# Output slots of a store-bound pairwise product: four of 83 pairs in place of three of 124

## The chip, the cores and the metric

One core of a Trainium2 chip. The metric is the device time of one execution in microseconds (us). "The profile" is one execution recorded by the hardware profiler; "the packet records" are the trace's list of single DMA packets with start, duration, size and queue (it does not name the engine), from which I worked out what the views do not show.

## The reference

For 4,096 rows of 32 fields of 64 numbers, each field is multiplied by one 64x64 matrix, and every pair (i, j) of fields with i < j gives a product, element by element: 496 pairs a row, 520 MB of fp32 output from 34 MB of input.

```python
def reference(r_x, L0_rec_W):
    vid = jnp.einsum('bfd,de->bfe', x, W)
    idx_i, idx_j = jnp.triu_indices(32, k=1)
    return x[:, idx_i, :] * vid[:, idx_j, :]
```

## The kernel before

The 4,096 rows are 16 tiles of 256. A tile's input is 128 partitions x 32 fields x 128 numbers; its output 128 partitions x 496 pairs x 128 numbers, 512 bytes a pair and partition. TensorE makes `vid`, VectorE multiplies, SyncE's queue stores, and ScalarE's queue loads the next tile in four DMAs of 512 KB. The first stores are cut by the list GROWING, since VectorE has no lead over the DMA yet.

```python
SLOT = 124
GROWING = [21, 15, 19, 23, ...]          # (cut) pairs of each early store
xpool = tc.tile_pool(name="x", bufs=2)   # (cut) two input tiles
opool = tc.tile_pool(name="out", bufs=3) # (cut) three output slots
...
def load(t, pieces, queue):
    xt = xpool.tile([P, F, C], F32, tag="x", name=f"x_{t}")
    n = F // pieces
    for lo in range(0, F, n):
        queue.dma_start(out=xt[:, lo : lo + n, :], in_=x[t][:, lo : lo + n, :])
    return xt
loaded = [load(0, 4, nc.sync), load(1, 2, nc.sync)]
...
for t in range(NT):
    if 0 < t < NT - 1:
        loaded.append(load(t + 1, 4, nc.scalar))
    ...                                  # matmuls of tile t into 8 PSUM banks
    for j in range(1, F):
        i = 0
        while i < j:
            at = first(j) + i
            base = at - at % SLOT
            if at == base:
                ot = opool.tile([P, SLOT, C], F32, tag="o", name=f"o_{t}_{at}")
            n = min(j - i, base + SLOT - at)
            nc.vector.tensor_tensor(ot[:, at - base : at - base + n, :], ...)
            i += n
            at += n
            if t * NP + at == until or at in (base + SLOT, NP):
                nc.sync.dma_start(out=out[t][:, sent:at, :],
                                  in_=ot[:, sent - base : at - base, :])
                sent = at
                ...                      # until += next(growing)
```

A store moves one row per partition. In the packet records each row is one packet: 63,488 bytes for 124 pairs, 128 packets a store. Each DMA also leaves 16 packets of 4 bytes and 9 ns (2,320 for the 145 DMAs of a run), which I take for the completions of the 16 DMA engines; so I count 8 rows of a store for each engine. A load packet is 4,096 bytes (8 fields).

## Time and profile before

| | before |
|---|---|
| time, median of the first 3 runs | 1298.64 us (1297.97 to 1299.37) |
| stores / later loads | 82 / 56 |
| VectorE busy | 1098.1 us |
| moved | 553.81 MB, 427 GB/s over the span |

The prediction shows the lines that say what bounds the kernel. One more view: the windows of the last microseconds. Columns: stretch and its length, busy time of PE, weight loads, VectorE and POOL, the clock, the busy share of the DMA engines, GB/s.

```profile
1280.00:1284.00 4.00, 0.00 (x0) 0.00 (x0) 0.00 (x0) 0.00 (x0) 0.50 0.88 381
1284.00:1288.00 4.00, 0.00 (x0) 0.00 (x0) 0.00 (x0) 0.00 (x0) 0.50 0.22 95
1288.00:1292.00 4.00, 0.00 (x0) 0.00 (x0) 0.00 (x0) 0.00 (x0) 0.50 0.15 63
1292.00:1296.00 4.00, 0.00 (x0) 0.00 (x0) 0.00 (x0) 0.00 (x0) 0.50 0.07 32
```

A share of 0.07 is about one engine of 16. Half of the engines are done by 1284 us, and for another 11 us the run waits for the others, in the end for two or one. By the packet records the 16 engines write their completions of the last store between 1282.9 and 1295.1 us. I call the difference between first and last, 12.2 us, the **spread**, and the amount by which the slowest engine ends after the mean of the 16 its **lag**, 9.1 us here. (The prediction's 1283.7 and 1295.9 are the same completions, counted from a zero 0.8 us earlier than the profile's. It also calls "lag" what is here the spread, as do the expectations ahead of the runs.)

### The profile page before, as it was taken

To read this page: it belongs to the slowest core of one execution; us is meant where nothing else is said; L and a number is where in the kernel's file an instruction comes from. 1 tells how busy PE (TensorE), PEld (TensorE's weight loads), DVE (VectorE), ACT (ScalarE), POOL (GpSimd) and SP (SyncE) were. 2 spreads that over 40 slices of the span, in tenths; PEclk is the share of its full clock that TensorE was granted. 3 is DMA by queue.
4 is the path that set the end of the run, shared out by engine and by line. 5 is a ranking of instruction groups with operands and counts; after the bars stand their busy time and mean duration, and the time that the engine had idled before them with its cause. 6 is when DMAs were issued, how large, how long until landed. Compare 5 with 4: busy or idle time off the path is not lost.

```text
span 1296.3 us, 2062 instructions
## 1 busy us (share of the span) xinstructions
PE 225.5 (17%) x512; PEld 52.1 (4%) x512; DVE 1098.1 (85%) x544; POOL 0.2 (0%) x4
## 2 busy tenths in 40 slices
PE   4112131122121121211212112121121211212000
PEld 1000000000000000000000000000000000000000
DVE  7999999898798888988888888888888888979970
POOL 0000000000000000000000000000000000000000
PEclk8555555565555555655555565555555655555555
DMA  9999999999999999999999999999999999999996
GB/s 379 430 426 433 438 432 425 434 434 434 428 432 432 434 432 434 431 434 436 432 434 434 426 434 432 430 432 432 432 433 431 434 432 434 432 431 443 425 431 288
DMA packets 20891, 553.81 MB, mean 427 GB/s; under 512 B 2448, under 2 KB 2448, under 8 KB 10256
## 3 DMA queue, kind: packets, MB, share of 16 engines
q1 hardware_dynamic: 12816, 524.33, 93.8%
q10 hardware_dynamic: 8064, 29.36, 5.5%
q8 instruction: 4, 0.07, 0.0%
q14 instruction: 7, 0.06, 0.0%
HBM read 33.59 MB, written 520.09 MB: 427 GB/s over the span
## 4 chain that ended last, share of the span: by engine, by line
DMA 61%; DVE 34%; issue 1%; DVEq 0%; PE 0%; SPq 0%
DMA out_dram<-o 61%; DVE o L99 34%; DMA x<-in_r_x_dram 0%; DVEq L145 0%; PE pv L81 0%; DVEq L99 0%; SPq L56 0%
## 5 line engine op out<-in xcount | busy, mean ns | idle before, releaser
L99 DVE TENSOR_TENSOR o<-x,pv 128x2176 f32<-128x2176 f32 (+27 forms) x544 | 1098.1, 2093 | 158.3 <-DMA out_dram<-o 149.5
L81 PE MATMUL pv<-x,w 64*64 64x512 f32 x512 | 225.5, 1025 | 966.3 <-DMA x<-in_r_x_dram 887.2
L81 PEld LDWEIGHTS pv<-x,w 64*64 64x64 f32 x512 | 52.1, 208 | 1138.0 <-issue 1137.4
L128 POOL MEMSET const-bfloat16-1.0<- 128x1 bf16 x1 | 0.1, 102 | 0.0
L128 POOL MEMSET const-uint8-127<- 128x1 uint8 x1 | 0.1, 102 | 0.0
L128 POOL MEMSET const-float32-1.0<- 128x1 f32 x1 | 0.1, 99 | 0.0
L128 POOL MEMSET const-float32-0.0<- 128x1 f32 x1 | 0.1, 98 | 0.2 <-issue 0.2
## 6 DMA issues: line engine op xcount, KB each, us to landing
out_dram<-o SPq DMA_DIRECT2D x56, 7936.0 KB, 42.9
x<-in_r_x_dram ACTq DMA_DIRECT2D x56, 512.0 KB, 48.7
out_dram<-o SPq DMA_DIRECT2D x2, 3008.0 KB, 17.8
out_dram<-o SPq DMA_DIRECT2D x1, 5952.0 KB, 27.1
out_dram<-o SPq DMA_DIRECT2D x1, 4928.0 KB, 23.1
out_dram<-o SPq DMA_DIRECT2D x1, 4416.0 KB, 19.0
out_dram<-o SPq DMA_DIRECT2D x1, 4224.0 KB, 21.2
out_dram<-o SPq DMA_DIRECT2D x1, 3904.0 KB, 15.3
```

The source lines that it names most:

```text
L81: nc.tensor.matmul(pv[half, :, :], lhsT=w2[half, :], rhs=xt[half, b : b + BANK, :], start=True, stop=True,)
L99: nc.vector.tensor_tensor(ot[:, at - base : at - base + n, :], xt[:, i : i + n, :], vid[j // BANK][:, j % BANK : j % BANK + 1, :].to_broad ...
L128: nc = _bacc.Bacc("TRN2", target_bir_lowering=False, num_devices=1, dynamic_dma_scratch_size=1024)
```

## The change

It cuts the output into slots of 83 pairs, of which four take less memory than the three before (332 pairs against 372), and re-cuts the early stores. Its evident intent is a finer flow: VectorE waits for smaller stores, with more of them in flight.

```diff
-SLOT = 124
+SLOT = 83
 GROWING = [
-    21, 15, 19, 23, 27, 19, 29, 18, 19, 20, 38, 28, 24, 25, 47, 34, 29, 61,
-    55, 69, 66, 58, 77, 47, 93, 31,
+    21, 24, 21, 17, 22, 15, 16, 30, 24, 20, 21, 18, 27, 24, 32, 46, 37, 50,
+    31, 45, 38, 53, 30, 65, 18,
 ]
-    opool = ctx.enter_context(tc.tile_pool(name="out", bufs=3))
+    opool = ctx.enter_context(tc.tile_pool(name="out", bufs=4))
```

## The prediction

> **What bounds the kernel now.** I read the page first (slices, chain, groups), then the waits, then windows of the run's two ends, and last the trace's records of single DMA packets.
>
> ```profile
> DVE  7999999898798888988888888888888888979970
> DMA  9999999999999999999999999999999999999996
> GB/s 379 430 426 433 438 432 425 434 434 434 428 432 432 434 432 434 431 434 436 432 434 434 426 434 432 430 432 432 432 433 431 434 432 434 432 431 443 425 431 288
> DMA 61%; DVE 34%; issue 1%; DVEq 0%; PE 0%; SPq 0%
> L99 DVE TENSOR_TENSOR o<-x,pv 128x2176 f32<-128x2176 f32 (+27 forms) x544 | 1098.1, 2093 | 158.3 <-DMA out_dram<-o 149.5
> ```
>
> Each column is 32.4 us. The DMA engines are full in all but the last; VectorE is busy in eight or nine tenths, and nearly all its idle time (149.5 of 158.3 us) ends when a store of an earlier output slot lands. The chain of waits says 34% VectorE, but that is how the chain is followed (slot freed, multiply, store, next landing). VectorE is not the limit: it waits for slots that the DMA empties.
>
> ```profile
> 100.00:232.00 132.00, 26.05 (x56) 5.38 (x56) 130.92 (x65) 0.00 (x0) 0.53 1.00 431
> 232.00:1200.00 968.00, 174.42 (x384) 40.66 (x384) 824.15 (x409) 0.00 (x0) 0.54 1.00 433
> 1200.00:1256.00 56.00, 0.00 (x0) 0.00 (x0) 51.41 (x20) 0.00 (x0) 0.50 1.00 435
> 1280.00:1296.00 16.00, 0.00 (x0) 0.00 (x0) 0.00 (x0) 0.00 (x0) 0.50 0.33 143
> ```
>
> These are windows: stretch, length, PE, weight loads, VectorE, POOL, clock, DMA share, GB/s. Up to 232 us VectorE computes without a break and builds its lead (the sized first stores); from 232 us on 144 us of 968 are waits. The DMA share is 1.00 to 1280 us, then a third. In the packet records all 16 DMA engines have a packet in flight at every moment from 13 to 1280 us. The last store's 16 completions run from 1283.7 to 1295.9 us: eleven engines finish by about 1286, two at 1295. So **the end is set by the slowest of 16 always busy DMA engines**: its bytes, its packets, and the stalls peculiar to it.
>
> The sum for a fast engine: 553.65 MB / 16 = 34.60 MB. A 63,488-byte packet takes 2,342 ns (median), one of 4,096 bytes 159 ns, so 36.76 ps a byte plus 8.5 ns. On one engine a packet starts 3 to 4 ns before the one ahead has ended, so the pitch has about 5 ns a packet; after a store's last packet the next starts some 6 ns later than otherwise (completion write). 34.60 MB x 36.76 ps = 1272.0 us; (82 stores + 62 loads + weights) x 8 packets x 5 ns = 5.8; 145 completions x 6 ns = 0.9; first bytes at 3.0; slow first loads 1.4 (21.9 us of excess over 16 engines before 33 us). Together 1283.1 us, against 1283.7 measured. The slowest engine adds 12.2 us.
>
> [...] a tile's four loads (issued together on the other queue, 32 packets of 4 KB per engine) take up to 82.1 us to land, which is 32 x (2.342 + 0.159) = 80 us, one small packet behind each large one. So loads are always in flight in the plateau. [...] 133.3 ns a pair and 148 ns fixed, of which 60 ns are pitch, as the next instruction starts 88 ns before the end.
>
> **The change, part by part.**
>
> *Stores.* The order comparison shows 30 more rows on SyncE: 112 stores against 82 (64 whole slots become 96; the sized ones are cut differently). Same bytes. Each engine handles 30 x 8 = 240 more packets x 5 ns = 1.2 us, and 30 completions x 6 ns = 0.2 us. This is on the path: **+1.4 us**.
>
> *VectorE.* A tile is cut at five borders, not three, so 32 more multiplies (544 to 576 in all): busy time 1098.1 + 32 x 0.148 = 1102.8 us; on the clock 32 x 60 ns = 1.9 us. All of it comes out of the 149.5 us of waiting: **0**.
>
> *Slots.* Buffered pairs 3 x 124 = 372 become 4 x 83 = 332. Today VectorE starts a slot when the store three back lands, with two stores (40 us, at 20.0 us each with a load in flight) still queued, and issues 17.1 us later. A fast engine, 12 us ahead, has 40 - 12 - 17.1 = 11 us of work left then. After: a slot takes VectorE 17.1 x 83/124 = 11.4 us; a packet 42,496 x 36.76 ps + 8.5 = 1,570 ns, a store 8 x (1.570 + 0.159) = 13.8 us with a load behind each packet, 12.6 without. Three queued are about 40 us; left for a fast engine 40 - 12 - 11.4 = 17 us. The queue runs dry in neither: **0**.
>
> *Loads.* 32 x 1.729 = 55 us to land instead of 80, then 25 us of each tile without a load. They were in time already (VectorE waits 8.8 us for PE in the whole run, all at the start): **0**.
>
> *First stores.* The first (21 pairs) is the same, issued at 12.18 us, first packet 13.25: 1.07 us from issue to packet. The second ends at pair 45 instead of 36: the multiply of 9 pairs ends at 15.55 (14.20 + 1.348), so its packet can start at 16.65; the engines run dry at 16.46 (where store two starts today). **Up to 0.2 us** is lost. The next: pair 66 ends at 18.47, so 19.57, and the queue lasts to 16.65 + 24 x 0.151 = 20.3. Going on so, with 0.133 us per pair + 0.06 per instruction for VectorE and 0.151 per pair for the DMA, the slack stays above 0.7 us to the end of the sized stores, from the third mostly more than before's (down to 0.2 us at its fifth).
>
> *Tail.* When VectorE ends, three full slots are left to drain today (1256.4 to 1295.9). After, four smaller ones. It ends when the bytes are out: **0**.
>
> Sum without the slow engines: 1298.64 + 1.4 + 0.2 = **1300.2 us**.
>
> *Slowest engine.* This is the term I can't derive. The spread between first and last completion of a store is 1.0 us at 76 us, 1.4 at 172, then grows to 12.7 at 1170, about 0.2 us per store, and stays flat (12.2) in the last stores, where no load runs; it did not grow before 76 us either, where none ran. [...] Three readings: it goes with load packets (same number: 0); with store issues during loads (6 x 55/80 = 4.1 a tile against 4: 0, or x1.5 = +6 us if any issue counts); with bytes stored while loads fly (x0.69: -3.5 us). I choose +1: **1301 us**.
>
> **The rivals.**
> - *Starvation takes the place of slot waits.* Against: the slacks above, and 16 of 16 engines busy in the present profile with less reserve. If the sized stores were wrong, each hole costs its length, 1 to 5 us in all.
> - *Per-store overhead counts in full* [...] Against: today's sized stores, small and many, run at 426 to 433 GB/s (the first columns), so a store behind another costs almost nothing.
> - *Finer slots let VectorE work earlier and shorten the run.* It does start each piece earlier, but what it produces waits in the queue; its 149.5 us of waiting are the sign of a lead, not of loss. Worth 0.
> - *The stalls follow the packet length or the issues*: -3.5 to +6 us, the main spread.
>
> **Range and chances.** Low: 1300.2 - 3.5 = 1296.7; high: 1300.2 + 6 = 1306. I take 1296.5 to 1306. The 2% borders are 1272.7 and 1324.6; below the first lies less than the sum of a fast engine alone, above the second only a cost that today's small stores don't show. Faster 0.01, same 0.97, slower 0.02.
>
> **What would show it.** Right: DMA slices at nine to the end; 112 store issues; plateau near 433 GB/s; VectorE busy about 1103 us with 140 to 160 us of waits for stores in more and shorter pieces; load pieces landing at some 14, 28, 42, 55 us (median 35); a hole of at most 0.3 us near 16.5; the last store's completions spread over 8 to 18 us. Wrong: a slice below nine in mid run, a plateau below 428 GB/s, VectorE waiting on PE for more than 20 us, or a first stretch with engines without packets.

The numbers of the kernel before's profile behind these steps: VectorE takes 2,948 ns for 21 pairs and 4,281 ns for 31, which gives the 133.3 ns a pair and 148 ns fixed; where it does not wait, the next instruction starts 81 to 87 ns (median 83, where the prediction has 88) before the end of the one ahead. Of 6,045 load packets between 232 and 1180 us, 88% start 2 to 5 ns before a store packet ends and 4% the same time before another load packet ends, so the two kinds take turns. That many stores behind each other cost little beyond their packets was an estimate of mine from the 426 to 433 GB/s of the early, small ones. And 200 of the 6,064 store packets of 63,488 bytes in that stretch took over 50 ns longer than the line of 36.76 ps a byte plus 8.5 ns (2.39 to 2.91 us, median 2.48); a store was issued during 36% of these 200, and during 11% of all.

## The result, and the profile after

The changed kernel took **1295.02 us** (median of 4 runs, 1294.66 to 1297.10) against 1298.76 for the kernel before; ratio 0.9975, 95% interval 0.9958 to 0.9992. Ratios here are the mean time of one kernel's fast runs over that of the other's of the same rounds, so not quite the ratio of the medians quoted. A second comparison, told below, gave 1295.07 against 1298.09, ratio 0.9979 (0.9964 to 0.9995). So the change is worth about 3 us, a quarter of a per cent. At the 2% border that is "the same", as predicted, but the time lies below the range of 1296.5 to 1306, and the sign was wrong.

First the page's slices, chain and main group of the changed kernel:

```profile
DVE  7999999888898888988888888888888888888970
DMA  9999999999999999999999999999999999999998
GB/s 376 427 410 434 434 433 434 431 433 431 434 431 433 431 432 433 432 431 435 432 431 433 432 435 426 437 427 433 434 430 435 430 431 436 428 436 431 438 431 348
DMA 66%; DVE 29%; issue 1%; DVEq 0%; PE 0%; SPq 0%
L99 DVE TENSOR_TENSOR o<-x,pv 128x640 f32<-128x640 f32 (+14 forms) x576 | 1102.4, 1984 | 151.3 <-DMA out_dram<-o 142.2
```

Nothing has moved between engines: the DMA is full to the last slice, VectorE is busy 1102.4 us (predicted 1102.8) and waits 142.2 us for stores (predicted 140 to 160). The plateau is at nearly the same GB/s. What differs is the last slice, 348 GB/s against 288, and the third, 410 against 426. The windows of the changed kernel, for the same stretches as the prediction's and for the end:

```profile
100.00:232.00 132.00, 22.86 (x48) 4.46 (x48) 128.76 (x69) 0.00 (x0) 0.50 1.01 433
232.00:1200.00 968.00, 177.92 (x384) 38.06 (x384) 833.05 (x435) 0.00 (x0) 0.53 1.00 432
1200.00:1256.00 56.00, 0.00 (x0) 0.00 (x0) 49.69 (x20) 0.00 (x0) 0.50 1.00 432
...
1280.00:1284.00 4.00, 0.00 (x0) 0.00 (x0) 0.00 (x0) 0.00 (x0) 0.50 0.96 415
1284.00:1288.00 4.00, 0.00 (x0) 0.00 (x0) 0.00 (x0) 0.00 (x0) 0.50 0.65 280
1288.00:1292.00 4.00, 0.00 (x0) 0.00 (x0) 0.00 (x0) 0.00 (x0) 0.50 0.12 52
```

The plateau is a hair slower (432 against 433 in the long window), and the engines are busy longer: 0.65 against 0.22 between 1284 and 1288 us. But then it is over, where before a few engines still worked until 1295. The packet records say the same in single numbers:

| completions of the last store, us | first | mean of 16 | last | spread | lag |
|---|---|---|---|---|---|
| before | 1282.9 | 1286.1 | 1295.1 | 12.2 | 9.1 |
| after | 1285.7 | 1287.8 | 1291.9 | 6.2 | 4.1 |
| after, second profile | 1285.4 | 1288.0 | 1292.9 | 7.5 | 5.0 |

The average engine ends 1.7 to 1.9 us **later**, as the sum of the prediction said (+1.4 for packets, +0.2 for the start). The slowest ends 2.2 to 3.2 us **earlier**, because its lag has halved. The run ends with the slowest. So the question for the experiments: why do a few engines fall behind, and what in the change makes them fall behind less?

One local loss is visible too. These are windows from 90 to 95 us, first of the kernel before:

```profile
90.00:95.00 5.00, 2.01 (x6) 0.85 (x8) 5.00 (x5) 0.00 (x0) 0.50 0.99 422
```

and of the changed one:

```profile
90.00:95.00 5.00, 3.68 (x8) 0.85 (x8) 5.00 (x4) 0.00 (x0) 0.57 0.99 346
```

The DMA share is the same 0.99 with a fifth less moved: packets took longer. I count as **excess** what a packet took beyond 8.5 ns + 36.76 ps per byte, the line through the medians of 4,096 bytes (159 ns) and 63,488 bytes (2,342 ns). Between 33 and 100 us it is 1.9 us per engine after against 0.7 before. That is the third slice's 410 GB/s; every profile of the changed kernel's slots shows 1.6 to 1.9 us there, and why these packets are slow stays open.

### The profile page after: what moved, and what is told of

The parts are those of the page before. It is cut to its first block, busy times and chain, and to the rows that moved or that the text cites. A ratio compares the mean times of both kernels' runs of the same rounds, so it can differ in the third digit from the quotient of the medians.

```text
span 1293.3 us, 2181 instructions
## 1 busy us (share of the span) xinstructions
PE 229.0 (18%) x512; PEld 49.5 (4%) x512; DVE 1102.4 (85%) x576; POOL 0.2 (0%) x4
## 4 chain that ended last, share of the span: by engine, by line
DMA 66%; DVE 29%; issue 1%; DVEq 0%; PE 0%; SPq 0%
DMA out_dram<-o 65%; DVE o L99 29%; DMA x<-in_r_x_dram 0%; DVEq L145 0%; PE pv L81 0%; DVEq L99 0%; SPq L56 0%
## 5 line engine op out<-in xcount | busy, mean ns | idle before, releaser
L99 DVE TENSOR_TENSOR o<-x,pv 128x640 f32<-128x640 f32 (+14 forms) x576 | 1102.4, 1984 | 151.3 <-DMA out_dram<-o 142.2
L81 PE MATMUL pv<-x,w 64*64 64x512 f32 x512 | 229.0, 1027 | 951.7 <-DVE o L99 500.2
L81 PEld LDWEIGHTS pv<-x,w 64*64 64x64 f32 x512 | 49.5, 205 | 1129.5 <-issue 1124.8
## 6 DMA issues: line engine op xcount, KB each, us to landing
x<-in_r_x_dram ACTq DMA_DIRECT2D x56, 512.0 KB, 31.9
```

The source lines that it names most:

```text
L81: nc.tensor.matmul(pv[half, :, :], lhsT=w2[half, :], rhs=xt[half, b : b + BANK, :], start=True, stop=True,)
```

## The experiments

There were two ways to read the halved lag: by what the change did to the *slots* (four, smaller), or by what it did to the *packets* (42.5 KB instead of 63.5 KB). And there were the loads, since in the kernel before the spread grew only while loads were running. I name kernels by their slots ("124" before, "83" after) and the edit.

### No later loads, on 124

The two tiles loaded first are used in turn. The result is wrong on purpose.

```diff
-            loaded.append(load(t + 1, 4, nc.scalar))
+            loaded.append(loaded[(t + 1) % 2])
```

> The kernel before with no loads after the first two tiles (the two loaded tiles are used in turn; the result is wrong on purpose). 56 loads fewer take 29.36 MB / 16 x 36.76 ps + 56 x 46 ns = 70 us off every engine. Theory L: the spread of the last store's completions is 1 to 2 us instead of 12.2, time about 1218 us, more than 70 us less. Theory S or I: spread about 12, 1228 us.

Measured in one look: 1220.42 us. Its windows at the end:

```profile
1208.00:1212.00 4.00, 0.00 (x0) 0.00 (x0) 0.00 (x0) 0.00 (x0) 0.50 1.03 444
1212.00:1216.00 4.00, 0.00 (x0) 0.00 (x0) 0.00 (x0) 0.00 (x0) 0.50 0.77 333
1216.00:1220.00 4.00, 0.00 (x0) 0.00 (x0) 0.00 (x0) 0.00 (x0) 0.50 0.00 0
```

From full to nothing within one window: all engines end together, spread 1.5 us. 78 us were saved where the loads' own work is 70; the other 8 are the lag. So the slow engines came with the loads (spread 12.2 us with them, 1.5 us without). Theory S, a lag from the stores alone, is out.

### Fewer and larger load packets, on both

```diff
-            loaded.append(load(t + 1, 4, nc.scalar))
+            loaded.append(load(t + 1, 1, nc.scalar))
```

> The kernel before (slots of 124), each later tile loaded by one DMA instead of four: 8 load packets of 16 KB per engine instead of 32 of 4 KB, so load packets lie among the stores for 8 x (2.34 + 0.61) = 24 us of each tile instead of 80. 42 DMAs fewer also save 42 x (8 x 5 + 6) ns = 1.9 us. Theory L (the slowest engine falls behind while load packets take turns with store packets, in proportion to that time): its lag falls from 12.2 to 4 or 5 us, time about 1289 us. Theory S (the lag goes with the length of the store packets or the slots, not with the loads): lag stays 12, 1297 us. Theory I (it goes with the number of DMA issues, 8 a tile to 5): lag about 8, 1293 us.

> The changed kernel (slots of 83), each later tile loaded by one DMA instead of four: load packets lie among the stores for 8 x (1.57 + 0.61) = 17 us of a tile instead of 55. 1.9 us fewer for packets. Theory L: the lag of the slowest engine falls from 6.2 to 3 or 4 us, time about 1290.5 us, so slots of 124 with one load (about 1289) are then no worse than slots of 83. Theory S: lag stays 6, 1293 us, and it stays 3 to 4 us ahead of the same edit on slots of 124. Theory I: (10 issues a tile to 7) lag 4.5, 1291.5.

On 124: 1308.07 us (1307.84 to 1308.94), ratio 1.0083 (1.0068 to 1.0097). On 83: 1304.04 us, ratio 1.0047 (1.0030 to 1.0064), 9 us slower than the changed kernel. All three theories had said faster or equal; **all were wrong**. The windows of 124 with one load show the opposite of a short lag:

```profile
1288.00:1292.00 4.00, 0.00 (x0) 0.00 (x0) 0.00 (x0) 0.00 (x0) 0.50 0.48 206
1292.00:1296.00 4.00, 0.00 (x0) 0.00 (x0) 0.00 (x0) 0.00 (x0) 0.50 0.26 111
1296.00:1300.00 4.00, 0.00 (x0) 0.00 (x0) 0.00 (x0) 0.00 (x0) 0.50 0.15 63
1300.00:1304.00 4.00, 0.00 (x0) 0.00 (x0) 0.00 (x0) 0.00 (x0) 0.50 0.07 32
```

The spread is 18.1 us. So it is not the *time* for which load packets lie among the stores that counts. The packet records give a better picture, though one of packets that were found together and not of a trial. For each full store packet between 232 and 1180 us I added up the time of the other engines' load packets that lay beside it:

| load time beside one store packet | kernel | packets | mean excess | over 50 ns |
|---|---|---|---|---|
| none | 124, one load | 4,507 | 1 ns | 0.3% |
| 2.0 to 2.5 us | 124 (before) | 2,301 | 3 ns | 1.6% |
| 4 to 6 us | 124 (before) | 102 | 48 ns | 31% |
| 8 to 12 us | 124, one load | 219 | 258 ns | 69% |

In these counts store packets are slow where many load packets of other engines lie beside them (48 ns of excess at 4 to 6 us), and most of all with packets of 16 KB (258 ns at 8 to 12 us). (That a slowed packet lasts longer, and so lies beside more, is too little to make this: 0.26 us on 2.34.) An engine that stores while most others load is, by this count, out of step with them. Load time alone is not enough: with the packets of 2.5 and 3 KB of the next experiment 26 store packets had over 4 us of it beside them, and none took 50 ns longer.

### Two loads of 8 KB packets on 124; six loads of 2.5 and 3 KB packets on 83

The first is the same edit with a 2; the second cuts unevenly:

```diff
-        n = F // pieces
-        for lo in range(0, F, n):
-            queue.dma_start(out=xt[:, lo : lo + n, :], in_=x[t][:, lo : lo + n, :])
+        cuts = [F * k // pieces for k in range(pieces + 1)]
+        for lo, hi in zip(cuts, cuts[1:]):
+            queue.dma_start(out=xt[:, lo:hi, :], in_=x[t][:, lo:hi, :])
...
-            loaded.append(load(t + 1, 4, nc.scalar))
+            loaded.append(load(t + 1, 6, nc.scalar))
```

> The kernel before with two loads a tile, load packets of 8 KB. With 4 KB packets it takes 1298 us, with 16 KB 1308 us. If the stalls grow with the size of the load packet: 1300 to 1304 us, some 300 slow store packets (200 and 366). If there is a step between the two sizes: 1297 or 1307.

> The changed kernel with each later tile loaded by six DMAs instead of four: 48 load packets per engine, 48 x (1.57 + 0.11) = 81 us, so load packets lie among the stores all of the time again, as in the kernel before, while the store packets stay at 42.5 KB. 28 DMAs more cost 1.3 us. Theory L: the lag grows from 6.2 to 9 or up to 12 us, time 1299 to 1302 us. Theory S: lag stays 6, 1296.3 us.

With 8 KB: 1301.32 us, scattered from 1296.44 to 1305.71, 277 slow store packets (over 50 ns; 200 with 4 KB, 366 with 16 KB). So their number grows with the size of the load packet, without a step. But the profile is of the fastest of these runs, 1296.44 us, and its lag is 6.6 us, less than the kernel before's 9.1: more slow packets do not always mean a longer lag. With 2.5 and 3 KB on 83: 1298.02 us, only 10 slow store packets against 83 and about 140 in the changed kernel's two profiles. Theory L is refuted here a second time: load packets lay among the stores all the time and the spread stayed at 6.5 us. But it did not fall either, with the slow packets nearly gone. Where these last microseconds come from I did not find. The time is 3 us above the changed kernel's: the average engine ended 2.0 us later (1.3 were for the added loads).

### Halved stores from the old slots

The slots stay at three of 124. Only the DMAs are cut in two.

```diff
                 if t * NP + at == until or at in (base + SLOT, NP):
+                    if t > 1:
+                        mid = (sent + at) // 2
+                        nc.sync.dma_start(
+                            out=out[t][:, sent:mid, :],
+                            in_=ot[:, sent - base : mid - base, :],
+                        )
+                        sent = mid
                     nc.sync.dma_start(
```

> The kernel before, three slots of 124 as they were, but from the third tile on each slot's store issued as two DMAs of 62 pairs, so that store packets are 31.7 KB. 56 stores more cost 56 x 46 ns = 2.6 us. Theory P (a store packet stalls where it lies beside load packets of other engines; what the change altered is the length of the store packets): stalls become rarer, lag of the slowest engine 6 us or less, time 1293 to 1296 us, about as good as the changed kernel without its slots. Theory D (what counts is four small slots in place of three large ones): lag stays near 12, 1300.5 us.

Measured: 1295.07 us (1294.53 to 1295.95), the very time of the changed kernel run beside it (1295.07), ratio 0.9980 (0.9964 to 0.9995). The windows at its end:

```profile
1280.00:1284.00 4.00, 0.00 (x0) 0.00 (x0) 0.00 (x0) 0.00 (x0) 0.50 0.98 421
1284.00:1288.00 4.00, 0.00 (x0) 0.00 (x0) 0.00 (x0) 0.00 (x0) 0.50 0.81 349
1288.00:1292.00 4.00, 0.00 (x0) 0.00 (x0) 0.00 (x0) 0.00 (x0) 0.50 0.24 103
```

Spread 5.0 us, lag 2.9. The average engine ends 2.8 us later than before (predicted 2.6 for 56 stores, so 50 ns a store). Theory D, that it is the small slots, falls. Theory P is right about the time, but one of its words is not: the stalls did **not** become rarer. There were 218 slow store packets against 200, and the excess of store packets in that stretch was 1.9 us per engine against 2.1. They were shared more evenly among the engines. The completions of the stores on the way show it: with halved stores the lag is 2.8 us at 495 us and 2.9 at the end, where in the kernel before it grows from 3.5 to 9.1 and in the changed kernel from 2.7 to 4.1.

### The changed kernel again, and with three slots

The unaltered changed kernel was run beside the halved stores.

> The changed kernel once more, unaltered, beside the kernel before on the same chip, since the kernel before was seen from 1294.2 to 1299.6 us in the last call. If the 3.7 us are the change's and not that of the few runs first compared: 1294 to 1296 us against 1297 to 1298.5, ratio 0.997 to 0.998. If they were luck: ratio 1.000 to 1.001 with the two ranges lying over one another.

It took 1295.07 us (1294.48 to 1295.95), beside 1291.74 to 1299.68 for the kernel before (median 1298.09). The gain holds, and the changed kernel is steadier: one of the 11 runs of the kernel before was faster than any of it.

```diff
-    opool = ctx.enter_context(tc.tile_pool(name="out", bufs=4))
+    opool = ctx.enter_context(tc.tile_pool(name="out", bufs=3))
```

> The changed kernel with three slots of 83 instead of four (249 pairs buffered instead of 332); packets, stores and loads as in the changed kernel. Theory P (the gain is from the length of the store packets): 1294.5 to 1296 us, the same as with four. Theory D (it is from the fourth slot): back to 1297 to 1300 us. It would also be slower if the engines ran dry, which would show as DMA slices below nine.

Measured: 1295.10 us, ratio 0.9982 (0.9969 to 0.9995), spread 6.4. The fourth slot gives nothing: with 249 pairs buffered instead of 332 the DMA is as full and the time the same.

### Which stores to halve

If what counts is the length of the packets *beside the loads*, it should matter which stores are cut. In 124 a tile's loads are issued as VectorE finishes the tile before, when that tile's third and fourth slot are the next to be stored. First halving only those, then only the first and second slot's:

```diff
-                    if t > 1:
+                    if t > 1 and base >= 2 * SLOT:     # b_half23
+                    if t > 1 and base < 2 * SLOT:      # b_half01
```

> Slots of 124, but only the third and fourth slot's stores of each tile from the third on are issued in halves of 62 pairs: 32 packets of 31.7 KB per engine and tile, just those that take turns with the 32 load packets. 28 stores more than before cost 1.3 us on every engine instead of 2.6. Theory P2 (the sum of the stalls stays, but the slowest engine's lag is some 4 to 5 turns of one load and one store packet, so it shrinks with the turn, 2.5 to 1.33 us): lag 4 to 7 us, 1292.5 to 1294.5 us, a little better than the changed kernel. If the packets away from the loads matter too: 1296 to 1298 us.

> Slots of 124, only the first and second slot's stores of each tile from the third on issued in halves. 28 stores more cost 1.3 us on every engine, as with the third and fourth slot's. By the kernel before's trace a tile's load packets take turns with the stores of the third and fourth slot first; now, with 16 long packets of those two, 16 of 31.7 KB of the next tile's first slot follow, so half of the turns stay long. If the length beside the loads is what counts: lag 8 to 11 us, 1297 to 1299 us. If any halving does it: 1294.5 to 1295.5 us.

Third and fourth: 1295.05 us, ratio 0.9980 (0.9968 to 0.9992), spread 7.0; as fast as with all halved, though not the little better that I had expected. First and second: 1298.81 us, ratio 1.0007 (0.9992 to 1.0022), spread 11.6, lag 8.1. The end of the latter looks like the kernel before's,

```profile
1284.00:1288.00 4.00, 0.00 (x0) 0.00 (x0) 0.00 (x0) 0.00 (x0) 0.50 0.37 159
1288.00:1292.00 4.00, 0.00 (x0) 0.00 (x0) 0.00 (x0) 0.00 (x0) 0.50 0.29 127
1292.00:1296.00 4.00, 0.00 (x0) 0.00 (x0) 0.00 (x0) 0.00 (x0) 0.50 0.11 48
```

and of the former, for the same stretches:

```profile
1284.00:1288.00 4.00, 0.00 (x0) 0.00 (x0) 0.00 (x0) 0.00 (x0) 0.50 0.33 143
1288.00:1292.00 4.00, 0.00 (x0) 0.00 (x0) 0.00 (x0) 0.00 (x0) 0.50 0.13 56
1292.00:1296.00 4.00, 0.00 (x0) 0.00 (x0) 0.00 (x0) 0.00 (x0) 0.67 0.00 0
```

Both add 28 stores and have the same slots; only the place of the short packets differs. It is a difference of degree: of the load time beside full store packets (between 232 and 1180 us), 84% lay beside short ones with the third and fourth halved, and 57% with the first and second. The number of slow store packets went with it, 100 in the one and 290 in the other against 200 before, so here, other than with all stores halved, the stalls did change. That the mixing of long and short packets does harm of its own in the second case is not ruled out. So short store packets helped here where 84% of the load time lay beside them. What a store costs is the same in all three kernels with halved stores: with the excess taken off, the average engine ends 48 to 51 ns later for each one added.

### Other ways to part loads and stores

Input rows 20,480 bytes apart instead of 16,384, in case all engines read the same place of the memory at once, which no trace had shown. This was tried on 124 and later on 83:

```diff
     NT, _, F, _ = x.shape
+    F = F - 8
...
+    x = _np.pad(x, ((0, 0), (0, 0), (0, 8), (0, 0)))
```

> The kernel before, with the rows of its input laid 20,480 bytes apart in memory instead of 16,384 (the loads move the same bytes). Theory A (load and store packets meet at the same places of the memory, because all engines read at addresses a power of two apart): stalls change a lot, most likely fall; lag 1 to 4 us, time 1288 to 1291 us. Theory R (the stall comes from the load packets' number and rate alone, wherever they read): nothing changes, lag 10 to 13, 1297 to 1298.5 us.

> The changed kernel with the rows of its input 20,480 bytes apart in memory. On the kernel before that gave 1296.2 against 1298.1 us, of which 0.65 us per engine came from less excess in the first 33 us, and left the lag at 12. If that adds to the change: 1293 to 1294.5 us, the best so far. If not: 1295 us.

On 124: 1296.24 us, ratio 0.9985 (0.9966 to 1.0004), which is not clear of noise; the spread stayed at 12.0 us and the slow packets at 188, so theory A as I put it falls. On 83: 1295.46 us, no better than the changed kernel, with a spread of 8.5 us and a lag of 6.1. Then the loads on the stores' own queue, which in the profile before moved its first stores in the order of issue (their packets start at 13.3 to 17.3 us, at 16.5 to 19.7, the third's from 18.8 on):

```diff
-            loaded.append(load(t + 1, 4, nc.scalar))
+            loaded.append(load(t + 1, 4, nc.sync))
```

> The kernel before, with the later tiles loaded from the stores' own queue: the load packets of a tile then follow one another (32 x 0.16 = 5 us) between two stores instead of taking turns with store packets for 80 us. If the stalls need load and store packets beside each other, only a lagging engine's last store packets meet the other engines' loads, for as long as it lags: lag 2 to 6 us, time 1288 to 1292 us. If a load costs the slow engines the same however it is placed: lag 12, 1298 us. It would be slower (over 1300) if the loads come too late for PE behind the queued stores.

Measured: 1296.32 us, ratio 0.9988 (0.9969 to 1.0007), so no clear gain. The spread is 5.5 us and slow store packets are down to 23, as expected, but the average engine ends at 1289.6 instead of 1286.1 us. What the slow engines gained, all engines lost. The packet records show where: the load packets, which took 159 ns almost without exception before, now took 4.4 us per engine more than that in all. The times expected, 1288 to 1292, were missed. Last, both remedies at once, all stores of 124 halved and six loads a tile:

> Slots of 124 with all stores from the third tile on in halves, and six loads a tile of 2.5 and 3 KB packets. Costs 2.6 + 1.3 us on every engine against the kernel before. Small load packets left nearly no slow store packets in the changed kernel (8 against 73 to 120), so P2 expects a lag of 2 to 5 us and 1293 to 1296 us. If the lag has another source once the stalls are gone, as its 6.5 us with six loads in the changed kernel hints: 5 to 7 us, 1297 us.

Measured: 1298.68 us, with one run at 1305.80; slow store packets down to 69, spread 4.7, but the average engine at 1291.9 us, 1.9 later than the 3.9 us charged for its packets. Too much cutting. No version tried beats the changed kernel clearly: halved third and fourth stores on the old slots equal it.

## Why the prediction was wrong

*What bounds the kernel*: right. The DMA is full in both, and the run ends with its slowest engine.

*Stores (+1.4), VectorE (0), slots (0), first stores (up to +0.2)*: right in kind and nearly in size. The average engine ended 1.7 to 1.9 us later, and stores added in other versions cost some 50 ns each, where 46 were predicted. The hole near 16.5 us is there but cost 0.02 us per engine. Three slots in place of four changed nothing. That the sum comes out so near is in part luck: an excess of 1.2 us between 33 and 100 us was not foreseen, and in the first profile fewer slow packets later took 0.8 us of it back.

*Loads (0)*: here the mechanism slipped. The load pieces land sooner, as predicted (median 35), from 48.7 us before

```profile
x<-in_r_x_dram ACTq DMA_DIRECT2D x56, 512.0 KB, 48.7
```

to 31.9 us after:

```profile
x<-in_r_x_dram ACTq DMA_DIRECT2D x56, 512.0 KB, 31.9
```

But "in time already" was not the whole of it, since the slow engines came with the loads (spread 1.5 us without later loads, 12.2 us with them).

*The slowest engine (+1)*: **this is the step that failed.** The prediction gave three readings and chose +1, a middle between readings of opposite sign. The lag moved by -4.1 to -4.9 us, and the spread fell to 6.2 and 7.5 us, the one sign of being right (8 to 18 us) that clearly failed. Halving all stores refutes the reading by issues, as more issues came with a smaller lag. The same run refutes the reading by number of load packets, which was the same in all kernels with four loads. The third reading, by the bytes stored while loads fly, had the right sign and most of the size (the sum would have been 1300.2 - 3.5 = 1296.7 us), but that would have been luck. One load a tile left a quarter as many store packets beside loads (8 in place of 32 per engine and tile), and the spread grew to 18.1 us; six loads on 83 brought the bytes stored beside loads back to the old number (48 x 42.5 KB against 32 x 63.5 KB), and the spread stayed at 6.5 us. So none of the three readings held. What the runs put in its place is narrower: with loads of 4 KB packets, the lag goes with the length of the store packets that take turns with load packets. It was 9.1 us with 63.5 KB (9.0 with padded rows), 3.9 to 5.0 with 42.5 KB (three profiles; 6.1 with padded rows), 2.9 and 4.9 with 31.7 KB (all stores halved, or the third and fourth slot's), and 8.1 where only 57% of the load time lay beside short packets. Most of these are single profiles, and the kernel before alone ran from 1291.7 to 1299.7 us, so only the step from 9 to 6 or less is to be trusted; the medians of the times say the same.

*What stays open.* Why the slowing gathers on a few engines, and less so with short packets, is not shown. A guess of mine that no run here tests: an engine in step with the others stores while they store; one out of step stores while they load, is slowed and stays out of step, and a shorter turn of load and store brings it back into step sooner. That the lag stops growing early with all stores halved fits this, but does not prove it. The packet list does not name the engines, so whether it is always the same ones is not known either. Six small loads left a spread of 6.5 us with hardly a slow packet, which this guess does not explain.

*The rivals*: starvation didn't come (no middle slice below nine), a large cost of each single store didn't either (some 50 ns for each one added), and finer slots were worth 0 in themselves, as three slots show. The last rival named, stalls that follow the packet length, was the one that came, with -4.1 to -4.9 us where -3.5 was allowed for it.

*Range and chances*: the border of 2% was never near, and 0.97 for "same" was sound. The lower end, 1296.5, allowed the third reading exactly and nothing beyond it.

## What to carry to other kernels

When the profile shows the DMA full, as it does here to the last slice, ask which of the 16 engines ends last, not only how many GB/s they reach: the windows of the last microseconds show a tail of one or two engines at once (a share of 0.07 from 1292 us on). Where loads and stores took turns on the engines, it paid to shorten the stores that lie beside loads (packets of 31.7 or 42.5 KB in place of 63.5: 1295.05 and 1295.07 us against 1298.17 and 1298.09) and to leave the others alone, as each store added cost the average engine some 50 ns. Loads were best at 4 KB: packets of 16 KB widened the tail (18.1 us against 12.2), and those of 2.5 and 3 KB cost more than they gained (1298.02 us against 1295.02 on 83). When a term can go either way, a middle between its readings is no forecast: each of the three here could have been put to the test by one small edit, and none of them held.
